# Transfers of blocks 104 to 117 are given waits for TensorE's marks of the next block, as those of blocks 9 to 103 have them

## The chip, the cores and the metric

The kernel runs on one core of one Trainium2 chip. Its time is the time of one launch on the device in microseconds (us); of several runs the median is taken.

## The reference

One layer of a graph network on 6,250 nodes of 64 features, with a residual and a layer norm. There are 206,250 edges: 100,000 pairs in both directions and one loop per node. `row` is an edge's source, `col` its destination, and the edges come sorted by destination.

```python
msg = concat([x[col], edge_attr], axis=1)            # 206250 x 128
h = relu(msg @ W1a.T + b1a)                          # 128 hidden
h = h @ W1b.T + b1b
sums = segment_sum(h, row, 6250)
counts = segment_sum(ones, row, 6250)
agg = sums / maximum(counts, 1)
z = relu(concat([x, agg]) @ W2a.T + b2a) @ W2b.T + b2b
out = concat([z, x]) @ Wr.T + br
return layernorm(x + out)
```

The edges come in order of destination and must be summed by source. The sum is the hard part: it is a sort of 206,250 rows.

## The kernel before, in words

Edges are taken in tiles of 128, and 13 tiles make a block; there are 124 blocks. For each block:

- **First layer.** TensorE makes the 13 tiles' hidden rows (`hidden`, matmuls at L1352), ten tiles first and the last three a little later; ScalarE applies relu to three or four tiles at a time and writes them to `orow` (L1355), a ring of four blocks.
- **Transfers.** GpSimd sends each of the 13 tiles to a table in DRAM with one indirect transfer, `rows<-orow,rowidx` (L1392, in `scatter`): each of the 128 rows (520 bytes) goes to a slot that belongs to its source node's bin. The slots come from counts that TensorE makes (`cnt_ps`, L1091 and L1092) and VectorE scans. Blocks 4 to 103 are joined: three, six or nine of their tiles are first sorted among themselves on TensorE (L1264 and L1277) and go in wider transfers (`quads<-orow,qidx`, L1363). Blocks 104 to 123 have 13 plain transfers each.
- **Sums.** SP reads rows of the table that are complete back into SBUF (`rt<-rows`, `rt<-quads`, L1454); VectorE makes one-hot tiles (`oh`, L1483), and TensorE multiplies them (L1502), which sums the rows by node. These are worked off in groups of up to 12 tiles, some groups in each block's loop, with the sums of blocks that lie several loops back. At the end, after the last block, the rest of the table is summed and the nodes' own layers follow.

The blocks form three epochs of 114, 8 and 2, each with a table of its own (`rows0` to `rows2`).

The order of instructions on TensorE, ScalarE, VectorE and SP is written out by hand: it is that of the loop over `k`. GpSimd's order is chosen by the scheduler, from what each transfer depends on. `scatter(k - LEAD)` stands in loop k, with LEAD = 2. For the blocks in `PACED`, a transfer also waits for a TensorE instruction of the next block's loop, so that it cannot be sent earlier. Which one, the table `pace` in `scatter` says. For a block without joined tiles (`j0` = 0) it comes to this: row 0 waits for first-layer tile 9 of the next block, row 7 for its tile 12, row 2 for `"first"` and row 11 for `"rest"`. These two names are written by every group of sums in a loop, `"first"` with its first half and `"rest"` with its second, so what remains is the last group of that loop. Row 9's mark, `"join0"`, exists only where the next block is joined, and the wait is left out elsewhere. No block below 104 has `j0` = 0 among those that are paced before the change.

Of the kernel before, what the change touches and what calls it, by code (L numbers as in the profile page):

```python
# [461 lines left out]
PRE, EVERY = 9, 3  # L462
# [8 lines left out]
JOIN_FROM, JOIN_TO = 4, 104  # L471
THRICE = tuple(range(9, 27, 2))
JOINS = 3 if THRICE else 2
PACED = range(PRE, JOIN_TO)
SIDES, ENATS, CHUNK = 2, 2, 3
ON_ACT = 1
FULLQ = (3, 6, 9, 11)
# [9 lines left out]
def fast_path(  # L487
# [259 lines left out]
    with (  # L747
# [609 lines left out]
        def scatter(k):  # L1357
# [32 lines left out]
            for j in range(j0, BLK):  # L1390
# [13 lines left out]
                later = (min(k + 1, NGR - 1), pace.get(j))  # L1404
                if k in PACED and later in done:
                    tc.add_manual_dep(
# [614 lines left out]
```

## Time and profile before

| | us |
|---|---|
| three runs | 2144.05, 2150.46 (median), 2161.01 |
| profiled execution | 2135.4 |
| its span, first to last instruction | 2133.6 |
| mean granted TensorE clock in it | 0.873 of full speed |

| engine | busy us | share of the span |
|---|---|---|
| PE (TensorE) | 1647.0 | 77% |
| DVE (VectorE) | 1376.9 | 65% |
| POOL (GpSimd) | 1153.9 | 54% |
| ACT (ScalarE) | 1105.6 | 52% |

A group's row gives its line, engine, operation, the tiles written and read with their shapes, the count, then busy time and the mean ns of one, and last the idle time of the engine just before these instructions with what ended most of it. "issue" is idle time in which the engine waited for nothing that the profile shows; "remote" is a release that the profile can't place. In a timeline each row has its start, its length, and in brackets the idle time ahead of it. Transfers on POOL are counted by the time that GpSimd takes to issue them. The last block's transfers start 2018.3 us into the span; the sums of the rest and the nodes' layers take what is left.

### The profile page before, as it was taken

How to read it: one execution, taken by the hardware profiler on the slowest of the kernel's cores; microseconds unless marked ns; L12 is line 12 of the kernel's file. 1: busy time of each engine (PE TensorE's matmuls, PEld its weight loads, DVE VectorE, ACT ScalarE, POOL GpSimd, SP SyncE). 2: the span in 40 equal slices, each digit the busy share in tenths (PEclk: the TensorE clock that was granted, in tenths of full speed). 3: DMA queues.
4: the chain of work that ended last, by engine and by line, in shares of the span. 5: the costliest groups of instructions: out<-in, count | busy, mean ns of one | idle time of the engine just before them, and what ended most of it. 6: DMA issues, size and time to landing. Idle time of an engine off the chain costs nothing.

```text
span 2133.6 us, 33410 instructions
## 1 busy us (share of the span) xinstructions
PE 1647.0 (77%) x10901; PEld 1452.3 (68%) x10901; DVE 1376.9 (65%) x3210; ACT 1105.6 (52%) x2246; POOL 1153.9 (54%) x1268
## 2 busy tenths in 40 slices
PE   5468788778888888888787888788666777677787
PEld 4356676667767777777777777677556666677676
DVE  5477677667666777777677777677645444454377
ACT  2257777766666666666566666666422222222007
POOL 6465556666555566656565565666644444455510
PEclk8589898889899999999899899999878877788799
DMA  6556676756656576555565555556676656656472
GB/s 163 162 184 219 223 240 231 258 175 211 190 176 200 176 226 198 166 177 183 164 180 185 159 174 164 181 173 184 192 242 175 170 175 182 185 178 178 149 217 65
DMA packets 243142, 396.32 MB, mean 186 GB/s; under 512 B 43621, under 2 KB 177895, under 8 KB 242703
## 3 DMA queue, kind: packets, MB, share of 16 engines
q1 hardware_dynamic: 162109, 225.24, 37.4%
q0 software_dynamic: 48240, 121.28, 16.3%
q10 hardware_dynamic: 32610, 47.58, 6.5%
q8 instruction: 89, 1.46, 0.3%
q14 instruction: 94, 0.77, 0.1%
HBM read 218.49 MB, written 175.44 MB: 185 GB/s over the span
## 4 chain that ended last, share of the span: by engine, by line
PE 61%; ACT 11%; issue 10%; another core or an unknown queue 8%; DVE 7%; DMA 2%; POOL 0%; ACTq 0%; DVEq 0%; SPq 0%; POOLq 0%
PE h_ps L1502 24%; PE h_ps L1264 11%; PE h_ps L1352 10%; PE h_ps L1277 9%; ACT rj L1269 2%; ACT rhs L1317 2%; ACT orow L1355 1%; ACT marks L1237 1%; ACT rhs L1315 1%; PE cnt_ps L1091 1%; PE cnt_ps L1092 1%; ACT orow L1280 1%; DVE marks L1232 1%; DMA rt<-rows 1%
## 5 line engine op out<-in xcount | busy, mean ns | idle before, releaser
L1392 POOL DMA_INDIRECT rows<-orow,rowidx x985 | 947.5, 962 | 787.0 <-ACT orow L1355 240.7
L1502 PE MATMUL h_ps<-rt,oh 128*128 128x129 f32 x4056 | 603.2, 303 | 147.3 <-issue 123.9
L1502 PEld LDWEIGHTS h_ps<-rt,oh 128*128 128x128 f32 x4056 | 555.6, 215 | 172.7 <-issue 149.9
L1355 ACT ACTIVATE orow<-h_ps 128x384 f32<-128x384 f32 (+1 forms) x287 | 153.7, 537 | 659.5 <-PE h_ps L1352 503.4
L1277 PE MATMUL h_ps<-mv,rj 128*128 128x130 f32 x1672 | 267.0, 313 | 156.1 <-ACT rj L1269 100.3
L1277 PEld LDWEIGHTS h_ps<-mv,rj 128*128 128x128 f32 x1672 | 237.8, 216 | 201.1 <-ACT rj L1269 121.4
L1264 PE MATMUL h_ps<-marks,side 128*128 128x512 f32 x1254 | 337.3, 418 | 28.5 <-ACT xr_now L1652 14.9
L1562 DVE TENSOR_TENSOR part<-part,h_ps 128x387 f32<-128x387 f32 (+2 forms) x249 | 122.4, 492 | 329.5 <-PE h_ps L1502 142.9
L1483 DVE TENSOR_TENSOR oh<-ramp,rt 128x768 f32<-128x768 bf16 (+3 forms) x440 | 320.9, 763 | 9.1 <-DMA rt<-rows 9.0
L1352 PE MATMUL h_ps<-mv,rhs 124*128 124x128 f32 x1970 | 297.4, 298 | 20.2 <-ACT orow L1355 11.3
L1264 PEld LDWEIGHTS h_ps<-marks,side 128*128 128x128 f32 x1254 | 241.1, 200 | 82.2 <-ACT xr_now L1652 16.0
L1352 PEld LDWEIGHTS h_ps<-mv,rhs 124*128 124x128 f32 x1970 | 267.3, 209 | 26.4 <-ACT orow L1355 11.8
L1363 POOL DMA_INDIRECT quads<-orow,qidx x209 | 200.5, 959 | 92.8 <-ACT orow L1280 41.4
L1232 DVE TENSOR_TENSOR marks<-quad_ramp,ramp 128x1024 fp32r<-128x1024 f32 x209 | 250.6, 1203 | 0.0
L1280 ACT ACTIVATE orow<-h_ps 128x260 f32<-128x260 f32 x418 | 143.4, 388 | 82.1 <-PE h_ps L1277 30.3
L1269 ACT COPY rj<-h_ps 128x512 f32<-128x512 f32 x209 | 118.0, 588 | 128.2 <-PE h_ps L1264 73.2
L1105 DVE TENSOR_SCALAR of_quads<-cnt_ps 128x98 bf16<-128x98 f32 x100 | 26.6, 266 | 244.2 <-PE cnt_ps L1095 105.4
L1238 ACT ACTIVATE marks<-marks,ones 128x512 fp32r<-128x512 f32 x209 | 150.9, 722 | 6.8
L1237 ACT ACTIVATE marks<-quad_ramp,z_act 128x512 fp32r<-128x512 f32 x209 | 149.4, 715 | 0.0
L1049 DVE TENSOR_TENSOR_SCAN had<-ramp,bins 128x400 bf16<-128x400 bf16 (+1 forms) x124 | 135.0, 1089 | 13.4 <-issue 0.9
L1315 ACT ACTIVATE rhs<-rhs,from_win 60x896 f32<-60x896 bf16 (+1 forms) x116 | 130.4, 1124 | 2.8
L1317 ACT ACTIVATE rhs<-rhs,ones 60x896 f32<-60x896 f32 (+1 forms) x116 | 130.2, 1123 | 2.9
(189 smaller groups left out, 1521.3 us busy)
## 6 DMA issues: line engine op xcount, KB each, us to landing
rt<-rows SPq DMA_DIRECT2D x138, 390.0 KB
rt<-quads SPq DMA_DIRECT2D x98, 390.0 KB
rhs<-in_edgeT SPq DMA_DIRECT2D x91, 224.0 KB
rt<-rows SPq DMA_DIRECT2D x103, 195.0 KB
enat<-in_edgeJ SPq DMA_DIRECT2D x91, 192.0 KB
rows<-orow,rowidx POOLq DMA_INDIRECT x985
rows<-padrow ACTq DMA_DIRECT2D x12, 1300.0 KB
quads<-padrow ACTq DMA_DIRECT2D x11, 1300.0 KB
```

Of the source, the lines that this page charges most:

```text
L1232: nc.vector.tensor_tensor(m[:, :n, :], all_q[:, None, :].to_broadcast([P, n, QUAD * P]), z[:, :n, None].to_broadcast([P, n, QUAD * P]), op ...
L1237: nc.scalar.activation(m[:, t, :], all_q, AF.Square, bias=z_acts[k][:, i * JOIN + t : i * JOIN + t + 1], scale=-1.0)
L1264: nc.tensor.matmul(ps, s[:, p, i * JOIN + t, :], m[:, t, :], start=t + p == 0, stop=t == JOIN - 1 and p == 1,)
L1277: done[k, f"join{i}"] = nc.tensor.matmul(ps[:, j, :], rj[:, (g0 + j) * P : (g0 + j + 1) * P], m, start=True, stop=True).ins.name
L1280: nc.scalar.activation(mrow[:, g0 : g0 + 2, :], ps, AF.Relu)
L1317: nc.scalar.activation(rhs[D:WIDE, :], rhs[D:WIDE, :], AF.Relu, bias=ones[D:WIDE, :1], scale=-1.0)
L1352: done[k, c] = nc.tensor.matmul(ps[:, j, :], rhs[:WIDE, of * P : (of + 1) * P], m[:WIDE, :H], start=True, stop=True).ins.name
L1355: nc.scalar.activation(orow_of(k, k0, n)[:, :, :H], ps[:, :n, :], AF.Relu)
L1363: s = nc.gpsimd.indirect_dma_start(out=qep.rows.rearrange("(q r) f -> q (r f)", r=QUAD), out_offset=bass.IndirectOffsetOnAxis(ap=qidx[:, q ...
L1392: s = nc.gpsimd.indirect_dma_start(out=ep_.rows, out_offset=bass.IndirectOffsetOnAxis(ap=rowidx[:, k % RING * BLK + j : k % RING * BLK + j ...
L1483: nc.vector.tensor_tensor(res[:, at_tile : at_tile + nb * n, :], ramp[:, None, :].to_broadcast([P, nb * n, P]), node[:, :, None].to_broadc ...
L1502: m = nc.tensor.matmul(of_bin(b), oh[:, at_tile, :], rt[:, j * n + t, : H + 1], start=t0 + t == st.lo[b], stop=t0 + t == st.hi[b] - 1,)
```

## The change

```diff
--- before.py
+++ after.py
@@ -471,7 +471,7 @@
 JOIN_FROM, JOIN_TO = 4, 104
 THRICE = tuple(range(9, 27, 2))
 JOINS = 3 if THRICE else 2
-PACED = range(PRE, JOIN_TO)
+PACED = range(PRE, 118)
 SIDES, ENATS, CHUNK = 2, 2, 3
```

PRE is 9, so `PACED` was blocks 9 to 103 and is now 9 to 117. Only GpSimd's order changes; the rows of TensorE, VectorE, ScalarE and SP are the same.

On GpSimd before, around blocks 103 (`orow3_144`) to 107 (the number at `orow` is the block's place in the ring of four, 104 being `orow0_141`; a multiplier counts equal transfers in a row):

```order
L1392 DMA rows0_64<-orow0_141,rowidx_105 125440x130 x2
L1392 DMA rows0_64<-orow3_144,rowidx_105 125440x130
L1392 DMA rows0_64<-orow0_141,rowidx_105 125440x130 x2
L1392 DMA rows0_64<-orow3_144,rowidx_105 125440x130
L1392 DMA rows0_64<-orow0_141,rowidx_105 125440x130 x9
L1392 DMA rows0_64<-orow1_142,rowidx_105 125440x130 x13
L1392 DMA rows0_64<-orow2_143,rowidx_105 125440x130 x13
```

With the change, at the same place, from block 104 to the start of 107:

```order
L1392 DMA rows0_64<-orow0_141,rowidx_105 125440x130 x2
L1392 DMA rows0_64<-orow3_144,rowidx_105 125440x130
L1392 DMA rows0_64<-orow0_141,rowidx_105 125440x130 x2
L1392 DMA rows0_64<-orow3_144,rowidx_105 125440x130
L1392 DMA rows0_64<-orow0_141,rowidx_105 125440x130 x5
L1392 DMA rows0_64<-orow1_142,rowidx_105 125440x130 x2
L1392 DMA rows0_64<-orow0_141,rowidx_105 125440x130
L1392 DMA rows0_64<-orow1_142,rowidx_105 125440x130 x2
L1392 DMA rows0_64<-orow0_141,rowidx_105 125440x130
L1392 DMA rows0_64<-orow1_142,rowidx_105 125440x130 x5
L1392 DMA rows0_64<-orow0_141,rowidx_105 125440x130 x2
L1392 DMA rows0_64<-orow2_143,rowidx_105 125440x130 x2
```

Four of block 104's transfers have moved out of its run: its rows 0 and 7 stand third and sixth among those of 105, behind two and four of them, and its rows 2 and 11 (the x2) behind all nine early ones of 105. Each block from 105 to 117 does the same to the next, with row 7 seventh from then on.

At the other end, from the start of block 118 (`orow2_143`) on, where `orow1_142` is block 117:

```order
L1392 DMA rows1_65<-orow2_143,rowidx_105 25088x130 x2
L1392 DMA rows1_65<-orow1_142,rowidx_105 25088x130
L1392 DMA rows1_65<-orow2_143,rowidx_105 25088x130 x3
L1392 DMA rows1_65<-orow1_142,rowidx_105 25088x130
L1392 DMA rows1_65<-orow2_143,rowidx_105 25088x130 x8
L1392 DMA rows1_65<-orow1_142,rowidx_105 25088x130 x2
L1392 DMA rows1_65<-orow3_144,rowidx_105 25088x130 x13
```

All 13 of block 118's own transfers stand in one piece with rows 0 and 7 of 117 among them; rows 2 and 11 of 117 come behind, and 119's 13 follow as before.

## The prediction

> **What bounds the kernel now.** I read the page's groups first, for the engine with the most work and for what it waits for.
>
> ```profile
> span 2133.6 us, 33410 instructions
> PE 1647.0 (77%) x10901; PEld 1452.3 (68%) x10901; DVE 1376.9 (65%) x3210; ACT 1105.6 (52%) x2246; POOL 1153.9 (54%) x1268
> L1392 POOL DMA_INDIRECT rows<-orow,rowidx x985 | 947.5, 962 | 787.0 <-ACT orow L1355 240.7
> L1502 PE MATMUL h_ps<-rt,oh 128*128 128x129 f32 x4056 | 603.2, 303 | 147.3 <-issue 123.9
> ```
>
> TensorE (PE) has most of the work, and the sums (L1502) are its largest group. Of the 147.3 us that it idled ahead of them, 123.9 are put down to "issue": it waited for nothing that the profile can name. The next question is where these lie, so I asked for TensorE's groups in a stretch whose transfers are paced (1200 to 1500 us), and in one of blocks 107 to 118, whose transfers are not (1600 to 1900 us).
>
> ```profile
> L1502 PE MATMUL h_ps<-rt,oh 128*128 128x129 f32 x564 | 78.5, 293 | 0.2 <-issue 0.2
> ...
> L1502 PE MATMUL h_ps<-rt,oh 128*128 128x129 f32 x1026 | 162.7, 312 | 85.7 <-issue 75.5 <-remote 7.3 <-DVE oh L1483 2.2
> ```
>
> 0.2 us against 75.5 us, in equal times: the unnamed waits belong to the unpaced blocks. There GpSimd (POOL) sends a block's 13 transfers in one run. These are the first and last of block 109's run, and the first of block 110's:
>
> ```profile
> 1658.97 0.96 POOL L1392 DMA_INDIRECT rows<-orow,rowidx  x1 [10.72 <-ACT orow L1355]
> 1660.23 0.96 POOL L1392 DMA_INDIRECT rows<-orow,rowidx  x1 [0.30 <-issue]
> ...
> 1674.12 0.95 POOL L1392 DMA_INDIRECT rows<-orow,rowidx  x1 [0.31 <-issue]
> 1688.07 0.96 POOL L1392 DMA_INDIRECT rows<-orow,rowidx  x1 [13.00 <-ACT orow L1355]
> ```
>
> One transfer each 1.26 us (15.15 us for twelve steps), then GpSimd idles 13.00 us until ScalarE (ACT) has the next block's first rows. The windows over three such runs (of 109, 111 and 119) show what TensorE does meanwhile; the columns are window, length, busy time with the matmul records, granted clock, DMA share, GB/s.
>
> ```profile
> 1659.00:1666.00 7.00, 6.77 (x61) 1.00 0.79 212
> 1666.00:1678.00 12.00, 2.99 (x13) 0.69 0.49 133
> 1678.00:1682.00 4.00, 3.64 (x17) 0.50 0.88 268
> 1714.00:1721.00 7.00, 7.00 (x64) 1.00 0.82 237
> 1721.00:1732.00 11.00, 4.97 (x20) 0.69 0.35 103
> 1949.00:1961.00 12.00, 6.26 (x27) 0.71 0.33 106
> ```
>
> For the first 7 us TensorE works at 61 and 64 records, 8.9 per us. After that it gets 13, 20 and 27 records in 11 to 12 us, 60 in 35 us, 1.7 per us, although the DMA engines are less busy than before (0.33 to 0.49 against 0.8). Then TensorE's own rows:
>
> ```profile
> 1673.12 0.37 PE L1502 MATMUL h_ps<-rt,oh 128*128 128x129 f32 x1 [1.03 <-issue]
> 1678.36 7.32 PE L1502 MATMUL h_ps<-rt,oh 128*128 128x129 f32 x38 [4.87 <-issue]
> 1685.52 0.31 PE L1091 MATMUL cnt_ps<-had,one_w 128*128 128x350 bf16 x1
> 1686.11 2.39 PE L1352 MATMUL h_ps<-mv,rhs 124*128 124x128 f32 x20
> ```
>
> It comes back for good at 1678.4, 3.3 us after the last transfer's end (1675.07), works off the block by 1685.7, and makes the next block's first rows from 1686.1; those start the next run at 1688.07. So a block here lasts as long as TensorE needs, its slow stretch included (blocks 109 and 110 start 29.1 us apart), and the slow stretch ends with the run.
>
> One block is different: 106. In the chain that ended last, its run (1577 to 1594) lies under a wait for data:
>
> ```profile
> 1578.70 18.72 DMA rt<-rows
> ```
>
> **The change part by part.** TensorE's, VectorE's, ScalarE's and SP's rows are unchanged. On GpSimd four of the 13 transfers of each of blocks 104 to 117 get a wait for a mark of TensorE in the next block: rows 0 and 7 for tiles 9 and 12 of that block's first layer, rows 2 and 11 for the first half and the rest of the last group of its sums.
>
> *Rows 0 and 7* are placed third and seventh (in 105's run sixth) in the next block's run. Their marks are early (above, the run began at 1688.07, while the first-layer rows ran from 1686.11 for 2.39 us), so I cost these waits at nothing; what covers them is that two, and at least five, transfers of 1.26 us stand ahead.
>
> *Rows 2 and 11* are placed behind the run, and their marks are the end of the block's sums. So a run of 13 becomes one of 11 (9 of its own block, 2 left from the one before), and two transfers follow when TensorE is nearly through with the block. The run ends 2 x 1.26 = 2.53 us earlier. If TensorE comes back at the same distance from the run's end, it works 2.53 us at 8.9 instead of 1.7 records per us, worth 2.53 x (1 - 1.7/8.9) = 2.05 us for each block. Blocks 105 to 117 are 13; without 106, whose time is the load's, 12 x 2.05 = 24.6 us.
>
> *Entry.* Block 104's run is 15 long today (two are left from 103) and will be 11:
>
> ```profile
> 1527.91 0.96 POOL L1392 DMA_INDIRECT rows<-orow,rowidx  x1 [3.42 <-ACT orow L1355]
> 1545.59 0.96 POOL L1392 DMA_INDIRECT rows<-orow,rowidx  x1 [0.30 <-issue]
> 1549.20 1.36 ACT L1355 ACTIVATE orow<-h_ps 128x512 f32<-128x512 f32 x3 [15.17 <-remote]
> 1549.85 1.65 PE L1352 MATMUL h_ps<-mv,rhs 124*128 124x128 f32 x6 [9.52 <-ACT orow L1355]
> ```
>
> Here ScalarE, too, sees the rows it needs only at 1549.20, 2.7 us behind the last transfer, and TensorE stands still for 9.52 us for it. With four transfers fewer both go on 4 x 1.26 = 5.05 us sooner: 5.05 us.
>
> *Exit.* Block 118's run becomes 15 (its own 13 and the two early ones of 117): the same price with the other sign, -2.05 us.
>
> *What queues behind the new waits.* Behind rows 2 and 11 in GpSimd's order stands only the next block's run, which waits for ScalarE's rows of that block, made later than these marks. The distance is the one above: sums end at 1685.7, run at 1688.07, 2.4 us; one transfer fits, with about 1.4 us of idle behind it. The loads of sorted rows that need blocks 104 to 117 come at least three blocks later, so ten to twenty us on two transfers of a block reach no load. Should the transfers delay the next run after all, the run would still be the shorter one, and each 1.26 us of delay costs at most 1.26 us of TensorE's slow stretch.
>
> The bounds of the disputed cost, the slow stretch: below, nothing is gained (the two late transfers count with the next run); above, half of it goes. I take the value between, at 2.05 us a block, since the paced stretch shows that short pauses of GpSimd are enough to keep TensorE at full rate:
>
> ```profile
> 1298.09 0.95 POOL L1363 DMA_INDIRECT quads<-orow,qidx  x1 [1.29 <-ACT orow L1280]
> 1306.93 0.96 POOL L1392 DMA_INDIRECT rows<-orow,rowidx  x1 [1.57 <-remote]
> 1317.32 0.96 POOL L1392 DMA_INDIRECT rows<-orow,rowidx  x1 [2.63 <-PE h_ps L1352]
> 1300.00:1400.00 100.00, 80.41 (x568) 0.95 0.54 170
> ```
>
> Pauses of 1.29 to 2.63 us lie between runs of at most six here, and a clock of 0.95 goes with them.
>
> The sum: 24.6 + 5.05 - 2.05 = 27.6 us off the profiled 2135.4 us (2133.6 us of span and 1.8 around it), 2107.8 us. The median of the three runs, 2150.46, is 15.1 us above the profiled one; with the same offset the change's median is **2123 us**.
>
> **The rivals.** *Nothing is gained (C).* The pause between the two late transfers and the next run is about 1.4 us, at the lower end of the pauses of the paced stretch, and those stood between shorter runs. If what slows TensorE needs longer to drain, 13 still go nearly in a row: then the 12 blocks give nothing, and the entry and exit leave 5.05 - 2.05 = 3.0 us, 2147 us. The Trainium skill has a rule for this side ("SBUF — State Buffer", section "SBUF: two separate sides"): engine ports and DMA ports cannot contend, and TensorE's reads never wait on anyone. By that rule a run of transfers could not slow matmuls and its length would not matter, which gives the time of this case; the rows disagree, since records fall from 8.9 to 1.7 per us inside each run.
>
> *The waits break the runs further (B).* TensorE's marks may be seen late during a run, as ScalarE saw its rows late at 1549.20. Then GpSimd itself halts at row 0 or 7, the run splits, and the slow stretch shrinks by itself. If half of the 12 us goes: 6 x (1 - 1.7/8.9) = 4.9 us, 12 times is 58, with 5.05 from the entry 63: 2087 us. Against it: both marks fall in the first 2.4 us of a run, while TensorE is still at full rate.
>
> *Slower: the block's turn pays (D).* The two late transfers fall on the one place where the engines wait for each other within a us or two: sums end, counts, first-layer rows, ScalarE's rows, next run. If marks are seen late behind them too, TensorE waits there. The nearest price is a wait of TensorE for ScalarE in the paced blocks, whose transfers do go on across that turn:
>
> ```profile
> PE h_ps L1277 <- ACT rj L1269: 100.3, 55, 5.3
> ```
>
> 5.3 us is the longest of 55. At that price in 13 blocks, 69 - 27.6 = 41 us are lost: 2192 us. It decides from 27.6 / 13 = 2.1 us a block; the mean of that row, 1.8 us (100.3/55), is just below, and would leave 2147 us or so. For it speaks how near the two are, against it that only two transfers, not a run of six, fall there.
>
> That the change does not do what it says can be left out for the waits (GpSimd's order does move), but half of them, rows 0 and 7, cost and give nothing of their own beyond their place.
>
> **How the numbers follow.** Likeliest is the sum, 2123 us, with 0.45, and its own range is 2108 to 2138. Nothing gained has 0.25, runs broken further 0.11, slower 0.19. The range reaches from B to just short of D's full price: 2085 to 2185. A measurement of this kernel tells about 1% (21.5 us) from no change: faster means below 2129, slower above 2172. Of the sum's 0.45, 0.38 lies below 2129; with B, faster has 0.49. The sum's other 0.07 and C make 0.32 for the same. D leaves 0.19 for slower.
>
> **What would show it.** Right: runs of 11 from block 105 on, a pair of transfers near the end of each block, TensorE back at full rate about 14 us after a run's start and not 16 to 19; "issue" ahead of L1502 in blocks 107 to 117 down by about a fifth; starts of runs some 2 us closer; ScalarE's wait in block 104 about 10 us, not 15.17. C shows as the slow stretch beginning 2 to 3 us earlier after a run's start; B as pauses inside the run of 11; D as waits of TensorE for ScalarE, or of its counts and first-layer rows, at the turn of a block that are not there now. The prediction is wrong if TensorE's slow stretch does not end with the run, or if a load of sorted rows turns up behind the two late transfers.

## Result, and the profile after

The change takes 2118.94 us (median of four runs, 2113.43 to 2135.72) against 2147.26 us before (four runs, one more than in the table above): a ratio of 0.9877, interval 0.983 to 0.993, or 28.3 us between the medians. Forecast were 2123 us and 27.6 us. Ratios here and below compare the runs in the faster of a kernel's two states, while medians are of all runs.

The page of the changed kernel, the same rows as before:

```profile
span 2111.6 us, 33441 instructions
PE 1648.5 (78%) x10901; PEld 1455.0 (69%) x10901; DVE 1376.4 (65%) x3210; ACT 1105.0 (52%) x2246; POOL 1153.6 (55%) x1268
L1392 POOL DMA_INDIRECT rows<-orow,rowidx x985 | 947.2, 962 | 769.4 <-issue 207.4
L1502 PE MATMUL h_ps<-rt,oh 128*128 128x129 f32 x4056 | 602.3, 303 | 126.4 <-issue 105.4
```

All engines are busy for as long as they were. The unnamed waits of TensorE ahead of its sums fell from 123.9 to 105.4 us, and that is most of the 22.0 us by which the span is shorter. In 1600 to 1900 us of the changed kernel the group of sums reads:

```profile
L1502 PE MATMUL h_ps<-rt,oh 128*128 128x129 f32 x1150 | 183.8, 315 | 73.2 <-issue 63.9 <-DVE oh L1483 7.3 <-PE h_ps L1502 0.7
```

1150 records instead of 1026 fit into 300 us, with 63.9 us of unnamed waits and not 75.5. GpSimd's timeline (start, length, idle time ahead) shows one block as forecast: eleven transfers in one run, a wait for TensorE's sums, the pair, 1.58 us of idle, the next run.

```profile
1699.45 0.96 POOL L1392 DMA_INDIRECT rows<-orow,rowidx  x1 [1.47 <-ACT orow L1355]
...
1712.07 0.96 POOL L1392 DMA_INDIRECT rows<-orow,rowidx  x1 [0.30 <-issue]
1719.28 0.96 POOL L1392 DMA_INDIRECT rows<-orow,rowidx  x1 [6.25 <-PE h_ps L1502]
1720.62 0.96 POOL L1392 DMA_INDIRECT rows<-orow,rowidx  x1 [0.38 <-issue]
1723.16 0.96 POOL L1392 DMA_INDIRECT rows<-orow,rowidx  x1 [1.58 <-ACT orow L1355]
```

The windows over two such runs (from 1675.6 and 1723.2) answer to those of before:

```profile
1675.00:1682.00 7.00, 7.00 (x65) 1.00 0.72 187
1682.00:1691.00 9.00, 3.69 (x18) 0.78 0.46 141
1723.00:1730.00 7.00, 6.69 (x59) 1.00 0.99 266
1730.00:1739.00 9.00, 3.59 (x12) 0.77 0.30 91
```

The slow stretch still begins 6 to 7 us into a run and has the same rate (30 records in 18 us), but it lasts 9 us instead of 11 to 12.

A window at a fixed time holds different work in two traces. To compare the same work I take the loops 107 to 116 of the program, from ScalarE's L1317 in loop 107 to that in loop 117. First the kernel before, then the changed one (window, length, TensorE's busy time and records, granted clock, DMA share, GB/s):

```profile
1610.20:1870.20 260.00, 180.77 (x1183) 0.78 0.61 175
```

```profile
1615.90:1843.10 227.20, 172.84 (x1177) 0.81 0.67 198
```

260.0 us became 227.2: 26.0 us a block became 22.7. Of the 32.8 us, 24.9 are idle time of TensorE (79.2 against 54.4) and 7.9 busy time, at a clock of 0.81 instead of 0.78.

### The profile page after: what moved, and what is told of

It is laid out like the page before. It is cut to its first block, busy times and chain, and to the rows that moved or that the text cites. A ratio compares the mean times of both kernels' runs of the same rounds, so it can differ in the third digit from the quotient of the medians.

```text
span 2111.6 us, 33441 instructions
## 1 busy us (share of the span) xinstructions
PE 1648.5 (78%) x10901; PEld 1455.0 (69%) x10901; DVE 1376.4 (65%) x3210; ACT 1105.0 (52%) x2246; POOL 1153.6 (55%) x1268
## 4 chain that ended last, share of the span: by engine, by line
PE 57%; issue 11%; DVE 10%; ACT 10%; another core or an unknown queue 8%; DMA 3%; POOL 1%; SPq 0%; ACTq 0%; DVEq 0%; POOLq 0%
PE h_ps L1502 22%; PE h_ps L1264 10%; PE h_ps L1352 9%; PE h_ps L1277 7%; DVE oh L1483 2%; DVE marks L1232 2%; ACT rhs L1317 2%; ACT rj L1269 1%; ACT orow L1355 1%; DMA rows<-orow,rowidx 1%; DMA rt<-rows 1%; ACT orow L1280 1%; ACT marks L1237 1%; PE cnt_ps L1091 1%
## 5 line engine op out<-in xcount | busy, mean ns | idle before, releaser
L1502 PE MATMUL h_ps<-rt,oh 128*128 128x129 f32 x4056 | 602.3, 303 | 126.4 <-issue 105.4
L1277 PE MATMUL h_ps<-mv,rj 128*128 128x130 f32 x1672 | 256.1, 305 | 136.3 <-ACT rj L1269 73.5
L1264 PE MATMUL h_ps<-marks,side 128*128 128x512 f32 x1254 | 343.7, 423 | 23.8 <-ACT xr_now L1652 10.6
L1277 PEld LDWEIGHTS h_ps<-mv,rj 128*128 128x128 f32 x1672 | 232.6, 210 | 174.4 <-ACT rj L1269 89.1
L1317 ACT ACTIVATE rhs<-rhs,ones 60x896 f32<-60x896 f32 (+1 forms) x116 | 130.2, 1123 | 2.9
```

Source lines behind the costliest of these rows:

```text
L1264: nc.tensor.matmul(ps, s[:, p, i * JOIN + t, :], m[:, t, :], start=t + p == 0, stop=t == JOIN - 1 and p == 1,)
L1277: done[k, f"join{i}"] = nc.tensor.matmul(ps[:, j, :], rj[:, (g0 + j) * P : (g0 + j + 1) * P], m, start=True, stop=True).ins.name
L1317: nc.scalar.activation(rhs[D:WIDE, :], rhs[D:WIDE, :], AF.Relu, bias=ones[D:WIDE, :1], scale=-1.0)
L1502: m = nc.tensor.matmul(of_bin(b), oh[:, at_tile, :], rt[:, j * n + t, : H + 1], start=t0 + t == st.lo[b], stop=t0 + t == st.hi[b] - 1,)
```

## The experiments

My theory, run length: on GpSimd only the number of transfers without a pause counts, since TensorE slows after some 6 us of it until shortly behind its end. Its rivals are named in the expectations. The runs fell on four chips. On three of them the kernel before takes 2145 to 2152 us, as in the prediction; on the fourth it takes 1608.65 us. The fourth came first. Each chip was used in one session alone, so it is not shown that the chip makes the difference and not something else in that session; "chip" below stands for both.

**One block only, and the fourth chip.** Edit (against the changed kernel):

```diff
-PACED = range(PRE, 118)
+PACED = range(PRE, JOIN_TO + 1)
```

> Only block 104 is paced, 105 to 117 are as before. Run length (my theory: what counts is the number of transfers that GpSimd sends without a pause): block 104's run has 11 instead of 15, 105's 15 instead of 13, so -5 + 2 = -3 us, ratio 0.998 to 0.999. Entry (rival: the change's gain is that of the one long run at the turn to unjoined blocks): most of the change's 28 us, ratio about 0.988.

Measured, on the fourth chip: 1608.43 us, ratio 1.0005 (0.9994 to 1.0016). Both ranges miss, since the ground on which the question stands is not there. Two windows of this kernel in its unpaced blocks, and the loops 107 to 116:

```profile
1282.00:1294.00 12.00, 12.00 (x109) 1.00 1.02 315
1294.00:1306.00 12.00, 12.00 (x109) 1.00 1.01 319
...
1259.60:1394.70 135.10, 132.80 (x1174) 1.00 1.03 313
```

GpSimd sends 306 transfers here without a pause (from 1158.7 to 1544.7 us), and in these loops TensorE does not slow: 9.1 records per us at a clock of 1.00, ten blocks in 135.1 us. The trace names what ended all but 2.1 us of the 43.9 us of its sums' idle time, most of it VectorE's one-hot tiles:

```profile
L1502 PE MATMUL h_ps<-rt,oh 128*128 128x129 f32 x4056 | 503.7, 279 | 43.9 <-DVE oh L1483 34.6
```

So what a long run does to TensorE is no property of the program alone; this chip does not show it. Nor is it all that sets the chips apart: loop 104 comes at 1204.0 us here and at 1531.9 us in the kernel before on its chip, so some 328 us of the difference lie ahead of the unpaced blocks. This kernel did not run on another chip. There the accounts by loops speak against its rival: the change's trace gains 32.8 us in loops 107 to 116, and 1.7 us from loop 104 to loop 107.

**Rows 2 and 11 alone, rows 0 and 7 alone.** The waits of blocks 104 to 117 are split in two halves (each added line is one of two kernels; `{...}` stands for the line taken out):

```diff
-else {j0: 9, j0 + 2: "first", 7: BLK - 1, 9: "join0", 11: "rest"}
+else {2: "first", 11: "rest"} if j0 == 0 else {...}      # rows 2 and 11 alone
+else {0: 9, 7: BLK - 1} if j0 == 0 else {...}            # rows 0 and 7 alone
```

> In blocks 104 to 117 only rows 2 and 11 wait, for the sums of the next block; rows 0 and 7 are free and stay in their own block's run. The run is 11 long, as in the change, but nothing in it can halt GpSimd. Run length: as the change within 6 us, ratio 0.985 to 0.991. Splitting (rival: the waits of rows 0 and 7 halt GpSimd inside the run, which gives TensorE its pause): no or little gain, ratio 0.996 to 1.000.

> In blocks 104 to 117 only rows 0 and 7 wait, for first-layer tiles 9 and 12 of the next block; rows 2 and 11 are free. A run is 13 long again, with two of the block before in it. Run length: nothing from blocks 105 to 117, 104's run 13 instead of 15 (-2.5), 118's 15 instead of 13 (+2), ratio 0.998 to 1.001. Splitting: as the change, ratio about 0.988.

Measured on the fourth chip: rows 2 and 11 alone 0.9992 (0.9983 to 1.0001), rows 0 and 7 alone 1.0006 (0.9996 to 1.0016). Each is within 0.1% of no change. For the first that is the rival's range and for the second run length's, but on a chip without the slow stretch they speak for neither. On a chip with the slow stretch (before 2145.65 us) the same two kernels again:

> The kernel of the earlier run in which only rows 2 and 11 wait, again. Where the kernel before takes about 2,150 us: run length 0.980 to 0.990, as the change (runs of 11 and a pair near the block's end); splitting (waits of rows 0 and 7 inside the run) 0.994 to 1.000. Where it takes about 1,609 us: 0.998 to 1.000 again, which tells nothing of the two.

> The kernel of the earlier run in which only rows 0 and 7 wait, again. Where the kernel before takes about 2,150 us: run length 0.996 to 1.001 (13 transfers stand in a row again); splitting 0.980 to 0.990. Where it takes about 1,609 us: 0.999 to 1.001 again, which tells nothing of the two.

Measured: rows 2 and 11 alone 2108.09 us, ratio 0.9839 (0.979 to 0.989); rows 0 and 7 alone 2136.56 us, 0.9973 (0.9936 to 1.0009). The loops 107 to 116 of the first and of the second:

```profile
1618.10:1840.70 222.60, 169.06 (x1158) 0.81 0.68 200
```

```profile
1607.40:1866.00 258.60, 177.93 (x1181) 0.79 0.60 175
```

Runs of 11 that wait for no mark give 22.3 us a block (two of them, in blocks 107 and 108, halt after nine transfers for ScalarE's last rows, 2.76 and 2.85 us). Runs of 13, two of them transfers that wait for TensorE, give 25.9. The place of the two late transfers makes the gain, the waits of rows 0 and 7 don't: splitting, the rival named in the expectations, falls.

**The change again.**

> The changed kernel itself. Where the kernel before takes about 1,609 us, as in the four runs so far, GpSimd sends 306 transfers without a pause and TensorE's sums wait for nothing unnamed, so shorter runs have nothing to save: ratio 0.999 to 1.003 (rival, the gain is there on every chip: 0.985 to 0.99). Where the kernel before takes about 2,150 us: 0.983 to 0.992 again.

Measured, on a chip where the kernel before takes 2148.41 us: 2110.92 us, ratio 0.9839 (0.980 to 0.988); loops 107 to 116 in 230.4 us. The condition "about 1,609 us" did not come up again, so the changed kernel itself has not run on the fourth chip.

**Shorter runs.** Four late rows in place of two; `"mid"` is the group of sums that ends at 60% of the next block's tiles (the lines that find it are left out):

```diff
+else {2: "mid", 4: "mid", 9: "rest", 11: "rest"} if j0 == 0 else {...}
```

> As the run in which rows 2 and 11 wait, but four rows of blocks 104 to 117 wait for the next block: 2 and 4 for the group of sums at 60% of its tiles, 9 and 11 for its last. Runs are 9 long instead of 13, four late ones behind. Where the kernel before takes about 2,150 us: run length, with the 3 to 3.7 us that runs of 11 gave each block, twice that: ratio 0.964 to 0.974. Joining (rival: four late ones run into the next nine, 13 in a row again): 0.983 or above. Where it takes about 1,609 us: 1.000 to 1.006.

Measured (before 2151.79 us): 2087.82 us, ratio 0.9719 (0.968 to 0.976). That is run length's range; joining is not the rule. The loops 107 to 116:

```profile
1608.00:1819.20 211.20, 166.16 (x1165) 0.85 0.72 212
```

With runs mostly of nine a block takes 21.1 us: 26.0, 22.7 and 21.1 us for 13, 11 and 9. The step from 11 to 9 gives less than the first. Some runs did join with late ones: in these loops two of 11 (from 1620.6 and 1789.3 us), behind them one of 14 (from 1829.7) and one of 15 (from 1861.6).

**Blocks 118 to 122 too** (`PACED = range(PRE, 123)`):

> Blocks 118 to 122 are paced too. Run length: five more blocks at 2.0 to 3.3 us and no run of 15 at block 118, 10 to 20 us less than the change, ratio 0.978 to 0.984. If the late blocks are limited by something else (their loads, or the sums behind the last block), the ratio stays at 0.987 to 0.989.

> Blocks 118 to 122 paced too, again. Where the kernel before takes about 2,150 us: run length 0.974 to 0.981 (five more blocks at 2 to 3.5 us, no run of 15 at 118); if the late blocks are limited by something else, 0.982 to 0.986 as the change. Where it takes about 1,609 us: 1.003 to 1.006 again.

Measured: on the fourth chip 1.0043 (1.003 to 1.006), a loss of 0.4%; where the kernel before takes 2151.79 us, 2099.22 us and 0.9755 (0.971 to 0.980), as run length had it. The same edit is a gain on one chip and a small loss on another. My range for the first of these runs was written with the slow stretch in mind and missed.

**Waits inside the block.** Rows 5 to 8 and 9 to 12 of blocks 104 to 122 wait for groups of sums of their own block (`PACED` ends at 122; the lines that name the marks are left out):

```diff
-later = (min(k + 1, NGR - 1), pace.get(j))
+later = (min(k + 1, NGR - 1), pace.get(j)) if j0 else (k, *(("none",) if j < 5 else (1, "first") if j < 9 else (3, "first")))
```

> Blocks 104 to 122: no wait for the next block; rows 5 to 8 wait for the first half of the second group of sums of their own block, rows 9 to 12 for that of the fourth. Runs are 5, 4 and 4 long where TensorE is behind GpSimd. Run length, where the kernel before takes 2,150 us: no run reaches the 6 to 7 us after which TensorE slows, blocks of 18 to 20 us instead of 25.8, ratio 0.94 to 0.96; rival (it is the number of transfers per time that slows TensorE): 0.98 to 1.00. Where it takes 1,609 us: the waits are over before GpSimd comes to them, 0.998 to 1.004.

Measured (before 2148.41 us): 2063.29 us, ratio 0.9604 (0.958 to 0.963). The ratio lies at the upper end of run length's range (0.94 to 0.96) and far from the rival's: blocks take 20.8 us (207.5 for ten), not 18 to 20. GpSimd's timeline says why. In most blocks there is one pause, not two:

```profile
1676.02 0.95 POOL L1392 DMA_INDIRECT rows<-orow,rowidx  x1 [5.38 <-ACT orow L1355]
...
1683.54 0.95 POOL L1392 DMA_INDIRECT rows<-orow,rowidx  x1 [1.51 <-PE h_ps L1502]
...
1692.37 0.95 POOL L1392 DMA_INDIRECT rows<-orow,rowidx  x1 [0.30 <-issue]
```

and the windows over it:

```profile
1676.00:1683.00 7.00, 7.00 (x56) 0.86 0.82 222
1683.00:1694.00 11.00, 8.40 (x66) 1.00 0.69 206
```

Runs are mostly 5 and 8 long, since the second mark is over when GpSimd comes to it. Still, with a pause of 1.51 us after five transfers, TensorE gets 66 records in the 11 us that follow, 6.0 per us, where the unpaced runs gave 1.1 to 2.3. It is no single case: counted in the trace, the 11 us that begin 7 us behind a run's first transfer hold 46 to 87 records in the eight blocks here with five transfers and a pause, and 12 to 24 in the eleven blocks of the kernel before, all from 1600 to 1880 us. A pause of this size resets most of what builds up.

Then the marks lie later (groups that end at 45% and 80% of the block's tiles), blocks 105 to 123 have them, and 104 is as in the change:

> As the run with rows 5 to 8 and 9 to 12 waiting within their own block, but the marks lie later (groups at 45% and 80% of the block's tiles), blocks 105 to 123 have it, and 104 is as in the change: no run of 15 at 104 and none of 17 at the end. Where the kernel before takes about 2,150 us: run length 0.940 to 0.955; if the spacing of the marks does not matter, 0.958 to 0.962. Where it takes about 1,609 us: 0.999 to 1.006.

Measured: 2058.74 us, median of six runs between 2033.11 and 2066.05. The ratio, 0.9511 (0.946 to 0.957), is that of the three shortest and lies within the range of run length; the medians of all runs give 0.9568, just outside it. In its trace, loops 107 to 116 take 208.6 us, no less than the 207.5 us above, so a gain from the later marks is not shown. Its median is the lowest on these chips; on the fourth chip it has not run.

## Why the prediction was right

**The bound, and the place of the gain: right.** The time went out of TensorE's unnamed waits, most of GpSimd's runs are 11 long, and the slow stretch follows the end of the run. The halves run apart show that the waits of rows 0 and 7 cost and give nothing to be measured (0.9973, with 1 in the interval) and rows 2 and 11 all of it. In single blocks rows 0 and 7 were not free, though: in the runs of blocks 106, 107 and 108 GpSimd halts where, by its order, one of them stands, for 1.78, 1.90 and 1.24 us:

```profile
1587.41 0.95 POOL L1392 DMA_INDIRECT rows<-orow,rowidx  x1 [1.78 <-remote]
...
1615.66 0.96 POOL L1392 DMA_INDIRECT rows<-orow,rowidx  x1 [1.90 <-PE h_ps L1502]
...
1629.54 0.96 POOL L1392 DMA_INDIRECT rows<-orow,rowidx  x1 [1.24 <-PE h_ps L1502]
```

And in blocks 116 and 117 late transfers did run into the next run (12 and 13 in a row, from 1811.1 and 1834.0 us), as the rival in which nothing is gained has it.

**The price of a block: too small.** The sum had 2.05 us. Loops 107 to 116 gave 3.3 us each (32.8 for ten), the change run again 3.0. Of the 32.8 us, 9.2 come from one block alone, that of loop 107, right behind the halt at 1615.66. That looks like the rival in which the waits break the runs further, and the sum had put such halts at nothing. It is not the rule: the other nine loops gave 2.6 us each. Nor is it shown that it takes row 7's wait, since the run in which only rows 2 and 11 wait has a loop as short (16.2 us, here 16.1), right behind a halt for ScalarE's rows (the 2.85 us above). The other nine loops, before and changed:

```profile
1635.51:1870.20 234.69, 162.65 (x1061) 0.78 0.61 174
1632.03:1843.10 211.07, 157.70 (x1059) 0.81 0.65 194
```

TensorE's idle time falls from 72.0 to 53.4 us, 2.1 us a block, which is the 2.05 of the sum. The rest, 0.5 us a block, is busy time, which the sum left out. In the change run again the nine loops gave 2.8 us each, 2.2 of it idle time. Whether the busy time belongs to the run length is open: in the kernel in which only rows 0 and 7 wait, with runs of 13 as before, it is 158.8 us in these loops. So the price that the sum had for the slow stretch held, and the terms that it had at nothing, halts and busy time, made the block's gain larger.

**The entry: right at its place, then lost.** Block 104 has 11 transfers, and ScalarE and TensorE went on sooner, by 5.5 and 5.8 us (forecast 5.05):

```profile
1551.15 1.36 ACT L1355 ACTIVATE orow<-h_ps 128x512 f32<-128x512 f32 x3 [9.71 <-remote]
1551.80 1.65 PE L1352 MATMUL h_ps<-mv,rhs 124*128 124x128 f32 x6 [3.71 <-ACT orow L1355]
```

But the next block runs into the load, which in the chain that ended last stands where it stood:

```profile
1579.91 17.08 DMA rt<-rows
```

It ends at 1597.0 us, before at 1597.4, though block 104 came 7.4 us later in this trace (loop 104's L1317 at 1539.3 against 1531.9). From loop 104 to loop 107 only 1.7 us are left of the 5.05 and of block 105's 2.05. I had left out the load for block 106 itself, and not seen that it can take back what is won ahead of it. In the change run again no such load stands in the chain there and 5.7 us are left, so this term varies from run to run. (Block 106's run before ends at 1592.8 us, not 1594; nothing hangs on it.)

**The exit.** Forecast was a loss of 2.05 us. From loop 117 to the end of the span the trace has a loss of 5.1 us, the change run again one of 0.5. The sum's sign holds, its size is within the scatter of single profiles.

In all, by the trace: 1.7 and 32.8 won, 5.1 lost, 29.4 us; and 7.4 us lost ahead of loop 104, where the program is the same (in seven other traces on such chips, of kernels that differ from the one before only behind it, loop 104 comes 1.1 to 22.4 us later than there), which leaves the 22.0 us of the spans. Terms too small and too large met, and that the sum of 27.6 us came so near to the 28.3 of the medians is luck: the change run again gave 37.5 us.

**The rivals.** That nothing is gained is out on these chips (0.9877 and twice 0.9839); a pause of 1.2 to 2.2 us between the pair and most next runs is enough. On the fourth chip the changed kernel did not run, but its halves gave nothing there (0.9992 and 1.0006). There TensorE keeps 9.1 records per us beside a DMA share of 1.0, which agrees with the Trainium skill's "SBUF — State Buffer", section "SBUF: two separate sides", that engine and DMA ports do not contend. Where the kernel before takes about 2,150 us the rows say otherwise: in the prediction's windows TensorE gets 1.7 records per us beside a share of 0.33 to 0.49. The slower case did not come: no wait of TensorE for ScalarE at a block's turn shows in the rows above.

What stays open is the cause of the slow stretch. That it needs a run of over 6 us, that a pause of 1.5 us resets most of it, and that one chip in four, in the one session on it, lacks it is shown; what is held up in it is not. Two causes can be set aside by the trace of the kernel before. The granted clock of 0.69 in the window 1666 to 1678 would leave some 6 records per us (an estimate, 0.69 times 8.9), and there were 1.1. And TensorE does not wait for its instructions to be loaded: between 1817 and 1838 us no packet of an instruction queue begins in the trace, and yet TensorE idles 3.13 and 5.70 us there and goes on for good at 1836.01.

## What to carry to other kernels

If an engine idles for nothing that the profile names, lay the windows of its records over the timelines of the other engines: the wait may follow a stretch of another engine's work, and its end. A pause put into that stretch can be worth more than the work it delays; here one of 1.5 us after five transfers in most of the late blocks brought 4% of the kernel's time. Time such an edit on more than one chip before it stays, since the same edit here was 2.5% faster on one and 0.4% slower on another.

## What the runs showed of the hardware

- On chips where the kernel before takes 2145 to 2152 us, TensorE falls from 9 matmul records per us to 1 or 2 when GpSimd has sent indirect transfers (128 rows of 520 bytes, one each 1.26 us) without a pause for 6.5 to 9.3 us, and comes back 0.9 to 3.8 us behind the last (blocks 107 to 116 of the kernel before). The DMA engines are less busy in it (a share of 0.30 to 0.49), not more.
- ScalarE, too, can wait long in it, for a release that the profile can't place: 15.17 us beside a run of 15, 9.71 us beside one of 11. TensorE's ten tiles for it end 13.2 us before it starts in the first case (1535.96 and 1549.20 us) and 7.0 us in the second.
- On one chip of the four on which the experiments ran, with such transfers in a row of 306, TensorE stays at 9.1 records per us and a clock of 1.00 in the loops looked at, with the DMA share at 1.0. The same program takes 1609 us there, 25% less than on the others.
